# Four buffers of queries, beta added a chunk later, and another split of the product sums in a sparse two-layer graph kernel

## The chip, the cores and the metric

The kernel runs on one core of a Trainium2 chip. The metric is the device time of one execution in microseconds (us), the median of several runs. The core has TensorE (PE) for matmuls and transposes, VectorE (DVE), ScalarE (ACT) and GpSimd (POOL), each with a queue of its own that is worked off in order, and SyncE (SP), which here only issues transfers. POOL also issues the indirect transfers: gathers and scatters whose rows are told by a list of indices.

## The reference

Two layers of graph attention over N = 2048 nodes, for a batch of B = 8 graphs that share one sparse adjacency matrix `adj`, with F = 256 features, H = 4 heads and D = 64 features a head. Cut to what matters:

```python
# layer 0
q, k, v = x @ Wq.T + bq, x @ Wk.T + bk, x @ Wv.T + bv          # split into 4 heads
scores = clip(q . k / sqrt(64), -10, 10); scores = -10 where adj == 0
attn = softmax(scores over each chunk of 256 nodes)              # 8 softmaxes a row
ctx = sum over chunks of attn @ v
y = layernorm(ctx @ Wo.T + bo + x) * gamma + beta
x = layernorm(x + y)
# layer 1
Wh = x @ W;  e = leaky_relu(Wh . a_src [row] + Wh . a_dst [column]), only where adj != 0
x = layernorm(x + elu(softmax(e) @ Wh))
```

A row of `adj` has few entries (up to 24 here), so the kernel gathers the neighbours of each node instead of computing all 2048 scores. The nodes that are not neighbours enter layer 0's softmax only through a constant, which is added in closed form.

## The kernel before, in words

The nodes are sorted by their number of neighbours and cut into NT = 16 tiles of 128 nodes, one node a partition. Tile t has room for `CAPS[t]` neighbours: 24, 14, 13, 12, 11, 11, 10, 10, 9, 9, 8, 8, 7, 7, 6, 5, together 164. The batch is cut into NG = 4 groups of G = 2 graphs. The kernel goes through these stages:

1. The table stage (to about 255 us in the profile): `edge_lists` finds each node's neighbours, while `tables(0, t)` computes keys and values (`kv_d`), queries and x + beta (`qx_d`, both halves of one row) of group 0 and stores them in DRAM.
2. Layer 0 for groups 0 to 3, 16 tiles each, in an order of tiles that goes 15, 13, ..., 1, 0, 2, ..., 14. During groups 0 to 2, `tables(g + 1, t)` makes the next group's tables, one tile at a time.
3. Layer 1 for the first pair of groups, woven into groups 2 and 3 of layer 0.
4. Layer 1 for the second pair, alone at the end.

**A tile of layer 0.** `fetch0` gathers the tile's neighbours. A *unit* is a buffer for UNIT = 2 neighbours of all 128 nodes, with keys in its first 512 columns and values in the next; there is a ring of RING = 14 such buffers (`tag="u"`). Each neighbour is one gather on POOL (L469), and one more (L507) brings the tile's own queries and x + beta into `qx`, of which there are 3 buffers. `scores0` multiplies queries and keys on DVE and sums each product over the features of a head. That sum is made in two ways. For the first `npe` units it goes over PE: DVE makes the product (L530), PE transposes it in eight pieces that add up in PSUM (L541), ACT copies the result (L547), and PE multiplies by a matrix of zeros and ones (L551). For the other units DVE makes the product (L555) and sums it with a reduce (L557). The product of unit i is written over the keys of unit i - 1, whose product was made before; the first unit's has a tile of its own, `prod`. `softmax0` clamps the scores (L571; PE's from PSUM, the others from SBUF), and makes the weights on DVE with one exponential on ACT. `context0` multiplies the values by the weights, most units on DVE (L481), the last quarter on ACT (L487), and sums them over the neighbours on PE (L494), which frees the ring's buffers. `finish0` applies Wo and the first layernorm and adds x + beta, which it reads from `qx` (L619 and L625); after L625 the `qx` buffer is free. `rows1` makes the tile's rows for layer 1.

**Tables.** `chunk_x` (L322) works on two tiles of x at once, every other tile: PE transposes x (L334), ACT copies it out as `xT` and `xC` (L336, L339). The `xt` tile of x, two buffers, then serves a second end: in `tables` of the odd tile POOL adds beta to it in place (L352), and it is stored in `qx_d`. Then it is loaded again by `load_x`, two tiles ahead.

**What sets the order.** The loop from L779 on writes out, for each tile k: the gathers of tile k + 1 (`fetch`), the scores of k, the rest of k - 1 and k - 2, the tables, then softmax and context of k. A planner then puts each engine's instructions in an order, by what it takes to be ready first; so the order on an engine is not that of the source, and a small edit can move many instructions. At run time every engine keeps that order: an instruction that waits holds up what is behind it. On POOL, that means that an add (L352) or a queries gather (L507) that waits holds up the gathers of units behind it.

Of the kernel before, what the change touches and what calls it, by code (L numbers as in the profile page):

```python
# [9 lines left out]
F32 = mybir.dt.float32  # L10
# [4 lines left out]
ALU = mybir.AluOpType  # L15
AX = mybir.AxisListType

P = 128
H = 4
D = 64  # L20
DP = 8
NJ = D // DP
# [14 lines left out]
G = 2  # L37
UNIT = 2
# [133 lines left out]
def sparse_path(ctx: ExitStack, tc: tile.TileContext, keep, x, adj, Wq, bq, Wk, bk, Wv, bv, Wo, bo, gamma, beta, W, a,  # L172
                out):
    nc = tc.nc
    B, N, F = x.shape
# [146 lines left out]
    def chunk_x(g, t):  # L322
# [18 lines left out]
        xTs[g, t] = xT, xC, xt  # L341
        return xT

    def tables(g, t):
        if t % 2 == 0:
            chunk_x(g, t)
        xT, xC, xt = xTs[g, t - t % 2]
        rows = slice(t % 2 * P, (t % 2 + 1) * P)
        if t % 2:

            xv = xt.rearrange("p k (b f) -> p (k b) f", b=G)
            nc.gpsimd.tensor_tensor(xv, xv, beta_r.unsqueeze(1).to_broadcast([P, 2 * G, F]), op=ALU.add)  # L352
            nc.sync.dma_start(qx_d[g][(t - 1) * P:(t + 1) * P, GF:].rearrange("(k p) f -> p k f", p=P), xt)
        kvs = work.tile([P, 2 * GF + 1], F32, tag="kvs", name="kvs", bufs=1)
        if g == PG:
            nc.scalar.copy(kvs[:, 2 * GF:], rank[:, t:t + 1])
        vk = kvs[:, 0:GF].rearrange("p (j b f) -> p b j f", b=G, j=NJ)
        for b in range(G):
            pm = bank("tk")
            for kc in range(KC):  # L360
                nc.tensor.matmul(pm[:, 0:F], xT[:, b * KC + kc, rows], wkv[:, kc, 0:F], start=(kc == 0), stop=False,  # L361
                                 skip_group_check=True)
            add_bias(pm[:, 0:F], biasT[:, 1])
            for kc in range(KC):
                nc.tensor.matmul(pm[:, F:], xC[:, b * KC + kc, rows], wkv[:, kc, F:], start=False, stop=(kc == KC - 1),  # L365
                                 skip_group_check=True)
            nc.scalar.copy(vk[:, b], pm[:, 0:F].rearrange("p (j f) -> p j f", j=NJ))
            nc.scalar.copy(kvs[:, GF + b * F:GF + (b + 1) * F], pm[:, F:])  # L368
        nc.sync.dma_start(kv_d[g][t * P:(t + 1) * P, :], kvs[:, 0:kv_d[g].shape[1]])
        q = bank("tk")  # L370
        for b in range(G):
            qb = q[:, b * F:(b + 1) * F]
            for kc in range(KC):
                nc.tensor.matmul(qb, xT[:, b * KC + kc, rows], wq[:, kc, :], start=(b == 0 and kc == 0), stop=False,  # L374
                                 skip_group_check=True)
            add_bias(qb, biasT[:, 0])
        qs = work.tile([P, GF], F32, tag="qs", name="qs", bufs=1)
        nc.scalar.copy(qs.rearrange("p (j b f) -> p b j f", b=G, j=NJ),
                       q.rearrange("p (b j f) -> p b j f", b=G, j=NJ))
        nc.sync.dma_start(qx_d[g][t * P:(t + 1) * P, 0:GF], qs)  # L380
        if t == NT - 1:

            tot = small.tile([P, G, KC], F32, tag="tot", name="tot", bufs=1)
            nc.vector.tensor_reduce(tot, xsum.pop(g), axis=AX.X, op=ALU.add)
            mv = small.tile([P, KC, G], F32, tag="mvs", name="mvs", bufs=1)
            pv = bank("tk")[:, 0:KC * G].rearrange("p (c b) -> p c b", c=KC)
            for oc in range(KC):
                for kc in range(KC):
                    nc.tensor.matmul(pv[:, oc, :], wkv[:, kc, F + oc * P:F + (oc + 1) * P], tot[:, :, kc],
                                     start=(oc == 0 and kc == 0), stop=(kc == KC - 1), skip_group_check=True)  # L390
            for oc in range(KC):
                nc.scalar.activation(mv[:, oc, :], pv[:, oc, :], AF.Identity, scale=-1.0, bias=bvc[:, oc:oc + 1])
            bO = small.tile([P, G, KC], F32, tag="bO", name="bO")
            po = bank("tk")[:, 0:KC * G].rearrange("p (c b) -> p c b", c=KC)
            for oc in range(KC):
                for kc in range(KC):
                    nc.tensor.matmul(po[:, oc, :], wo[:, kc, oc * P:(oc + 1) * P], mv[:, kc, :],
                                     start=(oc == 0 and kc == 0), stop=(kc == KC - 1), skip_group_check=True)
            for oc in range(KC):
                nc.scalar.activation(bO[:, :, oc], po[:, oc, :], AF.Identity, bias=biasT[:, 2, oc:oc + 1])  # L400
            biasO[g] = bO

    def first_tables(t):
        if t == 0:
            load_x(0, 0)
        if t % 2 == 0 and t + 2 < NT:
            load_x(0, t + 2)
        tables(0, t)

    with tc.tile_pool(name="lists", bufs=1) as pool:  # L410
# [92 lines left out]

    def fetch0(g, t):
        units = gather(kv_d[g].shape[1], kv_d[g], idx, t)
        qx = work.tile([P, 2 * GF], F32, tag="qx", name="qx", bufs=3)
        nc.gpsimd.indirect_dma_start(out=qx, out_offset=None, in_=qx_d[g],  # L507
                                     in_offset=bass.IndirectOffsetOnAxis(ap=node[:, t:t + 1], axis=0))
        got0[g, t] = qx, units

    def scores0(g, t):
# [2 lines left out]
        q = qx[:, 0:GF]  # L514
        sc = small.tile([P, GH, S], F32, tag="sc", name="sc")

        npe = len(units) - len(units) // 3
        ps_sc = bank("tf")[:, 0:GH * S].rearrange("p (s e) -> p s e", e=GH)
        W8 = GH * DP
        qv = q.rearrange("p (k j w) -> p k j w", k=UNIT, w=W8).unsqueeze(3)  # L520
# [1 line left out]
        def product(i):  # L522

            u, s0, n = units[i]
            if i:
                room = units[i - 1][0][:, :, 0:GF]
            else:
                room = work.tile([P, UNIT, GF], F32, tag="prod", name="prod", bufs=1)
            prod = room.rearrange("p k (j w) -> p k j w", w=UNIT * W8)[:, :, :, 0:n * W8]
            nc.vector.tensor_tensor(prod.rearrange("p k j (s w) -> p k j s w", w=W8),  # L530
                                    u[:, :, 0:GF].rearrange("p s (k j w) -> p k j s w", k=UNIT, w=W8),
                                    qv.to_broadcast([P, UNIT, NJ // UNIT, n, W8]), op=ALU.mult)
            return prod

        for i in range(0, npe, 4):
            some = units[i:min(i + 4, npe)]
            pr = bank("pr", 1).rearrange("p (k r) -> p k r", r=P)
            for k, (u, s0, n) in enumerate(some):
                prod = product(i + k)
                for j in range(NJ):  # L540
                    nc.tensor.matmul(pr[0:n * W8, k, :], prod[:, j // (NJ // UNIT), j % (NJ // UNIT), :], ident, is_transpose=True,  # L541
                                     start=(j == 0), stop=(j == NJ - 1), skip_group_check=True)
            m = len(some)
            prT = work.tile([P, 4, P], F32, tag="prT", name="prT", bufs=1)
            full = m - 1 if some[-1][2] < UNIT else m
            if full:
                nc.scalar.copy(prT[:, 0:full, :], pr[:, 0:full, :])  # L547
            if full < m:
                nc.scalar.copy(prT[0:W8, full, :], pr[0:W8, full, :])
            for k, (u, s0, n) in enumerate(some):  # L550
                nc.tensor.matmul(ps_sc[:, s0:s0 + n, :], prT[0:n * W8, k, :], sel[0:n * W8, 0:n * GH],  # L551
                                 start=(s0 == 0), stop=(k == m - 1 and i + m == npe), skip_group_check=True)
        for u, s0, n in units[npe:]:
            prod = u[:, :, 0:GF].rearrange("p s (j w) -> p s j w", w=W8)
            nc.vector.tensor_tensor(prod, prod, q.rearrange("p (j w) -> p j w", w=W8).unsqueeze(1)  # L555
                                    .to_broadcast([P, n, NJ, W8]), op=ALU.mult)
            nc.vector.tensor_reduce(sc[:, :, s0:s0 + n].rearrange("p e s -> p s e"),  # L557
                                    prod.rearrange("p s j (e d) -> p s e j d", d=DP),
                                    axis=AX.XY, op=ALU.add)
        st0[g, t] = ps_sc, sc, min(S, UNIT * npe)  # L560


# [3 lines left out]
    def softmax0(g, t):  # L566
        S = CAPS[t]
        n = GH * S
        ps_sc, sc, sp = st0.pop((g, t))
        for some, dots in ((sc[:, :, 0:sp], ps_sc[:, 0:sp, :].rearrange("p s e -> p e s")), (sc[:, :, sp:], sc[:, :, sp:])):  # L570
            nc.vector.tensor_scalar(some, dots, -10.0, 10.0, op0=ALU.max, op1=ALU.min)  # L571
        e = ebuf[:, 0:n]
        ev = e.rearrange("p (e s) -> p e s", s=S)
        nc.scalar.activation(ev, sc, AF.Exp)
# [198 lines left out]
            (fetch1 if layer else fetch0)(*at(i))  # L773
            fetched[0] += 1

    load_x(1, 0)
    fetch(0)
    waiting = None
    for k, (layer, i) in enumerate(seq):  # L779
# [6 lines left out]
        if layer == 0:  # L786
# [11 lines left out]
            if i:  # L798
                finish0(*at(i - 1))
            if g + 1 < NG:  # L800
                if i % 2 == 0 and i + NT + 2 < NG * NT:
                    load_x((i + NT + 2) // NT, (i + 2) % NT)
                tables(g + 1, i % NT)
            if tables_first:
                fetch(k + 1)
# [449 lines left out]
```

## Time and profile before

| | |
|---|---|
| time, median of 3 runs | 2462.93 us (2452.32 to 2464.49) |
| span of the profiled run | 2573.9 us |
| PE busy | 1940.6 us, 75% |
| DVE busy | 1833.1 us, 71% |
| POOL busy | 1505.4 us, 58% |
| ACT busy | 1408.0 us, 55% |
| mean granted clock of PE | 0.864 of full speed |
| moved by DMA | 669.10 MB, mean 260 GB/s |

The profiled run is longer than the timed ones, so times of the profile are compared with each other, and carried over to the timed runs by the ratio 2462.9 / 2573.9 = 0.957. A line of groups names the source line, the engine, the operation, what it writes and reads, the count, then the busy time in us and the mean of one instruction in ns, then the idle time of the engine just before such instructions and what ended it. A line of waits reads: who waited, for what, us in total, times, the longest.

### The profile page before, as it was taken

To read this page: it belongs to the slowest core of one execution; us is meant where nothing else is said; L and a number is where in the kernel's file an instruction comes from. 1 tells how busy PE (TensorE), PEld (TensorE's weight loads), DVE (VectorE), ACT (ScalarE), POOL (GpSimd) and SP (SyncE) were. 2 spreads that over 40 slices of the span, in tenths; PEclk is the share of its full clock that TensorE was granted. 3 is DMA by queue.
4 is the path that set the end of the run, shared out by engine and by line. 5 is a ranking of instruction groups with operands and counts; after the bars stand their busy time and mean duration, and the time that the engine had idled before them with its cause. 6 is when DMAs were issued, how large, how long until landed. Compare 5 with 4: busy or idle time off the path is not lost. (4 is left out here: it accounts for less than half of the span.)

```text
span 2573.9 us, 38911 instructions
## 1 busy us (share of the span) xinstructions
PE 1940.6 (75%) x11946; PEld 1657.1 (64%) x11946; DVE 1833.1 (71%) x4071; ACT 1408.0 (55%) x5011; POOL 1505.4 (58%) x1225
## 2 busy tenths in 40 slices
PE   6787787688878879989888877775856786555764
PEld 5675676577666767777777765664756675444654
DVE  5865567767557777767878797776877877656765
ACT  3573353355545455555555665654454567556756
POOL 1123655475545655655677667566757753667764
PEclk9888897898899999899999988886977887777877
DMA  6744977497877868887769878867769874986763
GB/s 217 261 154 159 330 254 256 149 336 254 292 259 243 279 221 307 294 299 271 264 239 369 293 276 299 302 230 250 230 212 338 306 260 178 346 306 236 279 243 108
DMA packets 240749, 669.10 MB, mean 260 GB/s; under 512 B 44455, under 2 KB 70826, under 8 KB 238486
## 3 DMA queue, kind: packets, MB, share of 16 engines
q0 software_dynamic: 156800, 505.01, 56.8%
q1 hardware_dynamic: 80016, 151.56, 16.1%
q10 hardware_dynamic: 3718, 9.97, 1.2%
q8 instruction: 98, 1.61, 0.2%
q14 instruction: 117, 0.96, 0.1%
HBM read 612.79 MB, written 126.36 MB: 287 GB/s over the span
## 5 line engine op out<-in xcount | busy, mean ns | idle before, releaser
L469 POOL DMA_INDIRECT u<-kv_d,idx x656 | 829.1, 1264 | 348.7 <-PE acc L494 161.0
L494 PE MATMUL acc<-ident,u 128*128 128x128 f32 x5248 | 745.0, 299 | 200.0 <-DVE u L481 97.0
L494 PEld LDWEIGHTS acc<-ident,u 128*128 128x128 f32 x5248 | 666.8, 156 | 267.1 <-DVE u L481 137.9
L469 POOL DMA_INDIRECT u<-wh_d,idx x328 | 402.6, 1228 | 166.0 <-issue 77.4
L481 DVE TENSOR_TENSOR u<-u,al 128x1024 f32<-128x1024 f32 x280 | 337.2, 1238 | 1.2
L481 DVE TENSOR_TENSOR u<-u,z 128x1024 f32<-128x1024 f32 x266 | 314.8, 1214 | 0.8
L487 ACT ACTIVATE u<-u,z 128x64 f32<-128x64 f32 x1008 | 259.0, 336 | 24.9 <-DVE z L678 10.6
L541 PE MATMUL pr<-ident,u 128*128 128x128 f32 x1472 | 208.7, 291 | 55.7 <-DVE u L530 49.3
L530 DVE TENSOR_TENSOR u<-u,qx 128x1024 f32<-128x1024 f32 x184 | 228.7, 1243 | 26.4 <-DMA u<-kv_d,idx 20.8
L541 PEld LDWEIGHTS pr<-ident,u 128*128 128x128 f32 x1472 | 179.0, 150 | 76.1 <-DVE u L530 64.3
L487 ACT ACTIVATE u<-u,al 128x64 f32<-128x64 f32 x800 | 206.9, 341 | 34.6 <-DVE al L585 15.2
L641 PE MATMUL mf<-wa,x1T 128*128 128x264 f32 x512 | 172.4, 465 | 63.0 <-issue 19.9
L352 POOL TENSOR_TENSOR xt<-xt,beta_r 128x1024 f32<-128x1024 f32 x32 | 80.2, 2508 | 217.0 <-PE tk L334 178.1
L507 POOL DMA_INDIRECT qx<-qx_d,node x64 | 81.4, 1272 | 185.6 <-DVE o L625 114.8
L361 PE MATMUL tk<-wkv,xT 128*128 128x256 f32 x512 | 154.6, 418 | 21.3 <-ACT xC L339 14.9
L641 PEld LDWEIGHTS mf<-wa,x1T 128*128 128x128 f32 x512 | 102.2, 221 | 103.8 <-issue 41.2
L374 PE MATMUL tk<-wq,xT 128*128 128x256 f32 x512 | 146.8, 404 | 28.1 <-ACT kvs L368 20.9
L613 PE MATMUL mf<-wo,cT 128*128 128x256 f32 x512 | 145.5, 408 | 6.3 <-ACT whs L644 4.5
L365 PE MATMUL tk<-wkv,xC 128*128 128x256 f32 x512 | 147.4, 404 | 0.0
L435 ACT ACTIVATE sq<-o,nm 128x256 bf16<-128x256 f32 x256 | 129.5, 506 | 5.0
L619 DVE CUSTOM_DVE_ANT_0 o<-mf,qx 128x256 f32<-128x256 f32 x128 | 49.2, 420 | 104.7 <-PE mf L311 93.9
L712 PE MATMUL mf<-ident,hT 128*128 128x128 f32 x256 | 51.4, 333 | 95.6 <-DVE xr L716 42.8
(168 smaller groups left out, 3434.5 us busy)
## 6 DMA issues: line engine op xcount, KB each, us to landing
kv_d<-kvs SPq DMA_DIRECT2D x48, 512.0 KB
wh_d<-whs SPq DMA_DIRECT2D x64, 260.0 KB
xt<-in_x_dram SPq DMA_DIRECT2D x64, 256.0 KB
qx_d<-xt SPq DMA_DIRECT2D x32, 512.0 KB
qx_d<-qs SPq DMA_DIRECT2D x64, 256.0 KB
x_d<-o SPq DMA_DIRECT2D x64, 256.0 KB
xr<-x_d SPq DMA_DIRECT2D x32, 512.0 KB
u<-kv_d,idx POOLq DMA_INDIRECT x656
```

Of the source, the lines that this page charges most:

```text
L361: nc.tensor.matmul(pm[:, 0:F], xT[:, b * KC + kc, rows], wkv[:, kc, 0:F], start=(kc == 0), stop=False, skip_group_check=True)
L365: nc.tensor.matmul(pm[:, F:], xC[:, b * KC + kc, rows], wkv[:, kc, F:], start=False, stop=(kc == KC - 1), skip_group_check=True)
L374: nc.tensor.matmul(qb, xT[:, b * KC + kc, rows], wq[:, kc, :], start=(b == 0 and kc == 0), stop=False, skip_group_check=True)
L435: nc.scalar.activation(sq, src[:, k, :], AF.Square, bias=nm[:, k:k + 1], accum_out=m2[:, k:k + 1])
L469: nc.gpsimd.indirect_dma_start(out=u[:, k, 0:width], out_offset=None, in_=table, in_offset=bass.IndirectOffsetOnAxis(ap=idx[:, t, s0 + k:s ...
L481: nc.vector.tensor_tensor(pv, pv, av, op=ALU.mult)
L487: nc.scalar.activation(pe, pe, AF.Copy, scale=al[:, e, s0 + k:s0 + k + 1])
L494: nc.tensor.matmul(acc[:, c, :], part[:, k, c * P:(c + 1) * P], ident, is_transpose=True, start=first and k == 0 and c == 0, stop=last and ...
L530: nc.vector.tensor_tensor(prod.rearrange("p k j (s w) -> p k j s w", w=W8), u[:, :, 0:GF].rearrange("p s (k j w) -> p k j s w", k=UNIT, w=W8),
L541: nc.tensor.matmul(pr[0:n * W8, k, :], prod[:, j // (NJ // UNIT), j % (NJ // UNIT), :], ident, is_transpose=True, start=(j == 0), stop=(j ...
L613: nc.tensor.matmul(po[:, b, :], cT[:, b * KC + kc, :], wo[:, kc, :], start=(b == 0 and kc == 0), stop=False, skip_group_check=True)
L641: nc.tensor.matmul(pw[:, 0:F + 2 * H], xT[:, b * KC + kc, :], wa[:, kc, :], start=(kc == 0), stop=(kc == KC - 1))
```

## The change

Four edits:

- `qx` has 4 buffers instead of 3.
- beta is added to a chunk of x when the next chunk begins (`add_beta`, called in `tables` two tiles later; the group's last chunk in its own last tile), where PE's transposes of that chunk lie further back. The load of the chunk after that is now issued in the same place, behind the add and its store.
- The first unit of each tile always has its product sums on DVE, so the tile `prod` is not needed any more; its 4 KB in each partition are those of the fourth `qx` buffer.
- The share of units whose sums DVE makes, a third before, is half in groups 0 and 1 (which have the tables beside them and no layer 1), and a sixth, at least one, in groups 2 and 3. The clamp of DVE's scores is split accordingly, since they now lie at both ends.

```diff
+    def add_beta(g, t):
+        xt = xTs.pop((g, t))[2]
+        xv = xt.rearrange("p k (b f) -> p (k b) f", b=G)
+        nc.gpsimd.tensor_tensor(xv, xv, beta_r.unsqueeze(1).to_broadcast([P, 2 * G, F]), op=ALU.add)
+        nc.sync.dma_start(qx_d[g][t * P:(t + 2) * P, GF:].rearrange("(k p) f -> p k f", p=P), xt)
+
     def tables(g, t):
         if t % 2 == 0:
+            if t:
+                add_beta(g, t - 2)
+            if g * NT + t + 2 < NG * NT:
+                load_x(*divmod(g * NT + t + 2, NT))
             chunk_x(g, t)
         xT, xC, xt = xTs[g, t - t % 2]
         rows = slice(t % 2 * P, (t % 2 + 1) * P)
-        if t % 2:
-            xv = xt.rearrange("p k (b f) -> p (k b) f", b=G)
-            nc.gpsimd.tensor_tensor(xv, xv, beta_r.unsqueeze(1).to_broadcast([P, 2 * G, F]), op=ALU.add)
-            nc.sync.dma_start(qx_d[g][(t - 1) * P:(t + 1) * P, GF:].rearrange("(k p) f -> p k f", p=P), xt)
+        if t == NT - 1:
+            add_beta(g, t - 1)
...
-        qx = work.tile([P, 2 * GF], F32, tag="qx", name="qx", bufs=3)
+        qx = work.tile([P, 2 * GF], F32, tag="qx", name="qx", bufs=4)
...
-        npe = len(units) - len(units) // 3
+        npe = 1 + len(units) - (len(units) // 2 if g < NG // 2 else max(1, len(units) // 6))
...
             u, s0, n = units[i]
-            if i:
-                room = units[i - 1][0][:, :, 0:GF]
-            else:
-                room = work.tile([P, UNIT, GF], F32, tag="prod", name="prod", bufs=1)
+            room = units[i - 1][0][:, :, 0:GF]
...
-        for i in range(0, npe, 4):
+        reduced(*units[0])
+        for i in range(1, npe, 4):
...
-        for u, s0, n in units[npe:]:
-...
+        for unit in units[npe:]:
+            reduced(*unit)
...
-        for some, dots in ((sc[:, :, 0:sp], ps_sc[:, 0:sp, :].rearrange("p s e -> p e s")), (sc[:, :, sp:], sc[:, :, sp:])):
-            nc.vector.tensor_scalar(some, dots, -10.0, 10.0, op0=ALU.max, op1=ALU.min)
+        nc.vector.tensor_scalar(sc[:, :, UNIT:sp], ps_sc[:, UNIT:sp, :].rearrange("p s e -> p e s"), -10.0, 10.0, op0=ALU.max,
+                                op1=ALU.min)
+        for some in [sc[:, :, 0:UNIT]] + ([sc[:, :, sp:]] if sp < S else []):
+            nc.vector.tensor_scalar(some, some, -10.0, 10.0, op0=ALU.max, op1=ALU.min)
```

The calls of `load_x` in `first_tables` and in the main loop (`load_x(1, 0)`, and the one at even tiles) are gone, since `tables` makes them.

## The prediction

> **What bounds the kernel now.** I read the page's busy shares first, then the windows cut where the layer 0 groups end (context copy L604: the 16th ends at 618 us, the 32nd at 1011, the 48th at 1521, the 64th at 2124), then the waits, the groups of instructions, and the landings behind the waits. Columns of a window are PE, PE weight load, DVE, ACT, POOL, clock, DMA share, GB/s.
>
> ```profile
> PE 1940.6 (75%) x11946; PEld 1657.1 (64%) x11946; DVE 1833.1 (71%) x4071; ACT 1408.0 (55%) x5011; POOL 1505.4 (58%) x1225
> 255.00:618.00 363.00, 283.35 (x1731) 242.07 (x1730) 242.91 (x449) 161.85 (x594) 211.06 (x172) 0.86 0.76 259
> 618.00:1011.00 393.00, 329.04 (x2054) 280.66 (x2053) 274.63 (x562) 202.57 (x793) 226.87 (x177) 0.93 0.78 269
> 1011.00:1521.00 510.00, 442.66 (x2848) 379.50 (x2846) 388.34 (x824) 293.27 (x1083) 337.21 (x253) 0.94 0.82 293
> 1521.00:2124.00 603.00, 433.18 (x2770) 373.24 (x2771) 469.01 (x1002) 336.12 (x1228) 394.37 (x313) 0.82 0.77 267
> ```
>
> Over the whole span no engine is full, but the stages differ. PE is busy 78%, 84% and 87% in groups 0, 1 and 2, which also hold the tables of the next group; DVE 67%, 70% and 76%. In group 3, without tables, DVE leads, 78% against 72%. So PE is the fuller engine before 1521 us and DVE after it, and both run in order, each with a fifth of its time lost to the other. The page's chain covers only the last 13 us and says nothing here.
>
> ```profile
> POOL u L469 <- PE acc L494: 223.1, 89, 19.0
> POOL xt L352 <- PE tk L334: 178.1, 11, 22.5
> POOL qx L507 <- DVE o L625: 114.8, 20, 19.1
> DVE prod L530 <- DMA qx<-qx_d,node: 26.1, 10, 9.7
> DVE prod L530 <- DMA u<-kv_d,idx: 25.4, 5, 10.7
> DVE u L530 <- DMA u<-kv_d,idx: 20.8, 10, 5.3
> ```
>
> POOL issues all gathers in order and waits at three places: for a ring buffer that PE frees (223 us), for the transposes ahead of x + beta (178 us) and for a queries buffer (115 us). But of the 178 us, the trace places seven waits (122 us) before 170 us, in the table stage, where POOL has nothing else to do. Only some 26 us of DMA lateness at queries and some 46 at units reach DVE's first products. POOL is not the bound; what it delays sometimes is.
>
> [...] 1243 ns for the product (L530), 1212 for the reduce (L557). A reduce thus costs as much as a multiply. [...] gathers with a DVE multiply beside most of them took 1.59 us on average, those with none 1.00. The change leaves the number of such multiplies alone. [...]
>
> **The change, part by part.** A group has 16 tiles and 86 units (12, 7, 7, 6, 6, 6, 5, 5, 5, 5, 4, 4, 4, 4, 3, 3). Before, a third of them, rounded down, is reduced on DVE: 24, and 62 go over PE. After, half, rounded down, in groups 0 and 1: 39 on DVE, 47 on PE. In groups 2 and 3 it is one a tile and two for the largest: 17 on DVE, 69 on PE.
>
> ```profile
> L541 PE MATMUL pr<-ident,u 128*128 128x128 f32 x1472 | 208.7, 291 | 55.7 <-DVE u L530 49.3 <-issue 5.8
> L541 PE MATMUL pr<-ident,prod 128*128 128x128 f32 x512 | 76.8, 290 | 48.9 <-DVE prod L530 39.2 <-issue 8.7 <-PE mf L641 0.8
> L551 PE MATMUL tf<-sel,prT 128*128 128x16 f32 x496 | 73.8, 278 | 29.8 <-ACT prT L547 18.4 <-issue 11.1
> L557 DVE TENSOR_REDUCE sc<-u 128x16 f32<-128x1024 f32 x64 | 77.4, 1212 | 0.2
> L557 DVE TENSOR_REDUCE sc<-u 128x8 f32<-128x512 f32 x32 | 21.8, 680 | 0.1
> ```
>
> PE, a unit: (208.7 + 76.8 + 73.8) us over 248 units is 1.45 us. The product is made on DVE on either path, so a unit moved to DVE adds only its reduce, 1.21 us (0.68 for a half unit). Groups 0 and 1, each: PE -15 x 1.45 = -21.8 us. DVE before 16 x 1.21 + 8 x 0.68 = 24.8, after 32 x 1.21 + 7 x 0.68 = 43.5, so +18.7, and a third clamp (L571's small form, 178 ns) in 14 tiles, +2.5: +21. That brings PE to 262 and 307 us and DVE to 264 and 296: level. Groups 2 and 3, each: PE +7 x 1.45 = +10.2. DVE saves little, since the last half units were the cheap ones: 17 x 1.21 = 20.6 instead of 24.8, -4.2. ACT gets four more copies of sums a group at 0.58 us; ACT is 58% busy and they lie beside products.
>
> What of this is on the path? Bounds: nothing, if each engine waits for the other as before; all, if PE alone set the time. I take half of PE's relief in groups 0 and 1, because DVE becomes as full: -22 us together (bounds 0 and -44). In group 2, at 87% PE, I take 7 of the 10 us; in group 3 PE has 170 us idle and DVE leads, so +1. Sum: -14 us.
>
> Four queries buffers: the wait L507 <- L625 goes for most tiles. In the order of the changed program most queries gathers have no DVE instruction left to wait for, and the first tiles' stand four together, then 39 units where 29 stood. Behind L507 on POOL are the next units; behind these DVE's first product. The ring keeps its 14 buffers, so POOL soon waits there instead, and the gain is only the lateness that reached DVE: 26 us of queries plus some part of the units'.
>
> x + beta a chunk later: the wait of L352 for the transposes of its own chunk goes. Orders compared: before, an add that waits for PE in groups 0 to 2 needs an instruction 8 to 67 places (median 18) ahead of the one that the next gather needs anyway; after, 8 to 148 (median 74). So it was mostly the ring's wait under another name. Three adds still stand ahead of the first gather, on the same transposes, so the start (first gather at 255.6 us although the first ring buffer is cleared at 224) stays. The load of x now goes out after the add and its store, but a buffer of x had to be stored before its reload already, and there are two as before; the order on SP in the table stage is the same. Cost nothing, hidden by PE's tables. The add itself, 2.4 us, stays.
>
> Without its own tile, the first unit's product takes its neighbour's room: no bytes, no time; the bytes pay for the queries buffer. But the first unit is now multiplied and reduced (2.45 us) before DVE makes PE's first product. PE can do tables, contexts and outputs meanwhile in groups 0 to 2.
>
> For queries and units together DVE waits 89 us on landings in these four stages by the trace, 17 of them at the start, which stay. Of the other 72 I take 30 as gone and two thirds of these as time: -20 (bounds 0 and -72). In all -34 us of the profiled 2574; the timed run is 2463, a factor 0.957: -32. **2463 - 32 = 2431 us.**
>
> **Rivals.** *Nothing to measure.* For: the ring sets POOL's lead before and after, and PE's relief equals DVE's load, 21.8 against 21. Against: PE is 11 to 14 points fuller in groups 0 and 1. Only some 8 us remain: 2455.
>
> *The late gathers were the path.* For: at tile t = 0 of group 0, L352 held POOL 18 us and DVE then waited 9.7 for queries, in a step of 60 us where group 1 takes 44. Against: 72 us is all that DVE waits there on landings. All 72, and PE's balance entire (-44 + 20): -96 x 0.957 = -92: 2371.
>
> *Slower.* PE's first product is later by 2.45 us in each of 64 tiles, 157 us; PE already waits for DVE's products (49.3 + 39.2 us above). In groups 2 and 3 PE gets 20 us more, and with no reduce left after PE's last product, DVE has less of its own to do while sums return. Against: the planner's order in the changed program puts other DVE work there (more of it than before in groups 1 and 2). If a quarter of the 157 shows, 39, and 10 in group 2, less 22 won: +27 x 0.957: 2489.
>
> **How the numbers follow.** Forecast 0.53, nothing 0.15, late gathers 0.12, slower 0.20. The threshold of 0.5% is 2451 and 2475. The forecast's own spread, -14 to -60 us, is faster throughout: faster 0.65, same 0.15, slower 0.20. The range goes from 2385, short of the centre of the late-gather case, to 2480, half of the slower one; about 2 in 10 lie outside.
>
> **What would show it.** Right: PE busy down by about 22 us in each of groups 0 and 1 and up by 10 in each of 2 and 3; 98 full reduces of 1.21 us and 14 half ones; L507's wait under 30 us in all and the ring's wait up by much of what goes; DVE's waits for queries near zero; groups 0 and 1 shorter by 10 to 20 us each, group 2 not shorter by PE work. Wrong: PE's waits for the first transposes grow by more than 30 us; the ring's wait stays while groups shrink (then POOL mattered more); groups 2 and 3 move by over 20 us (then the new order of the instructions, not these costs, decides).

## The result, and the profile after

The changed kernel takes 2430.6 us (median of 4 runs, 2418.3 to 2439.9) against 2463.7 us (2452.3 to 2473.2) before: a ratio of 0.986, 95% interval 0.981 to 0.991, or 33 us less. The forecast was 2431. Ratios here and below are of runs within 1.5% of the fastest of the same kernel; three of the later profiles (*head_qx*, *split_qx* and *split_beta*) are of slower runs, so times read in them are rough.

The profiled run of before that the prediction reads took 2573.9 us, 110 us more than the timed ones. The kernel before was profiled once more, unchanged, and that run took 2464.4 us; it is the one to set beside the 2438.2 us of the profile after, and it is called *control* from here on. Busy shares first, of control and then of after:

```profile
PE 1895.6 (77%) x11946; PEld 1622.3 (66%) x11946; DVE 1835.0 (74%) x4071; ACT 1404.5 (57%) x5011; POOL 1523.2 (62%) x1225
```

```profile
PE 1885.9 (77%) x11786; PEld 1610.9 (66%) x11786; DVE 1853.9 (76%) x4117; ACT 1400.3 (57%) x5029; POOL 1496.6 (61%) x1225
```

PE does 160 matmuls less and is busy 10 us less, DVE does 46 instructions more and is busy 19 us more. Neither comes near the 33 us of the result.

Next the windows, cut at the context copy of each group's 16th tile (L604 before, L613 after). Columns as in the prediction; the first number after the bounds is the window's length. Control, then after; groups 0 to 3, then the rest.

```profile
256.60:672.90 416.30, 341.88 (x2126) 291.21 (x2126) 293.09 (x558) 199.11 (x739) 263.14 (x210) 0.90 0.81 281
672.90:1075.80 402.90, 346.94 (x2207) 295.98 (x2206) 300.35 (x607) 220.23 (x864) 247.92 (x189) 0.94 0.80 282
1075.80:1505.50 429.70, 382.62 (x2525) 330.29 (x2523) 354.62 (x753) 261.51 (x954) 296.27 (x220) 0.95 0.83 299
1505.50:2023.10 517.60, 384.24 (x2540) 332.54 (x2541) 428.80 (x915) 309.85 (x1137) 372.83 (x294) 0.85 0.83 291
2023.10:2464.00 440.90, 256.46 (x1675) 224.65 (x1673) 294.25 (x728) 283.48 (x989) 284.52 (x236) 0.77 0.70 247
```

```profile
257.30:669.60 412.30, 339.23 (x1998) 285.21 (x1998) 308.65 (x597) 196.01 (x741) 259.64 (x208) 0.87 0.82 288
669.60:1065.50 395.90, 345.03 (x2095) 292.30 (x2094) 313.70 (x639) 221.40 (x873) 238.99 (x188) 0.91 0.80 283
1065.50:1491.70 426.20, 380.57 (x2530) 328.52 (x2528) 347.47 (x732) 258.78 (x955) 287.88 (x226) 0.94 0.85 305
1491.70:1999.10 507.40, 380.75 (x2615) 334.52 (x2615) 423.86 (x911) 308.14 (x1136) 366.92 (x289) 0.88 0.83 292
1999.10:2438.00 438.90, 253.49 (x1673) 219.82 (x1671) 293.74 (x729) 285.68 (x1000) 283.51 (x235) 0.77 0.70 249
```

The 26 us between these two profiles come in small pieces from everywhere: 4, 7, 3.5, 10 and 2 us. The largest piece is in group 3, which has no tables and where the change gave PE *more* work. The groups of instructions of after, counted by form (busy us, mean ns, then the idle time ahead):

```profile
L543 DVE TENSOR_REDUCE sc<-u 128x16 f32<-128x1024 f32 x98 | 118.4, 1211 | 0.3
L543 DVE TENSOR_REDUCE sc<-u 128x8 f32<-128x512 f32 x14 | 9.5, 676 | 0.0
L553 PE MATMUL pr<-ident,u 128*128 128x128 f32 x1712 | 250.6, 295 | 64.3 <-DVE u L534 54.9 <-issue 7.9 <-PE mf L650 0.8
L553 PE MATMUL pr<-ident,u 128*64 128x128 f32 x144 | 21.4, 285 | 0.0
L563 PE MATMUL tf<-sel,prT 128*128 128x16 f32 x428 | 63.1, 272 | 18.4 <-ACT prT L559 18.2
L563 PE MATMUL tf<-sel,prT 64*128 64x8 f32 x36 | 7.1, 269 | 0.0
L580 DVE TENSOR_SCALAR sc<-sc 128x16 f32<-128x16 f32 x74 | 13.3, 185 | 0.1
```

Now 112 reduces cost 127.9 us where 96 cost 99.2, and PE's part costs 250.6 + 21.4 + 63.1 + 7.1 = 342.2 us where it cost 354.5 in control (209.6 + 74.5 + 70.4). PE's idle time ahead of the transposes fell to 64.3 us, from 54.7 + 46.4 = 101.1. The waits on POOL, of control and then of after (us in total, times, longest):

```profile
POOL xt L352 <- PE tk L334: 179.5, 11, 25.0
POOL u L469 <- PE acc L494: 177.0, 106, 13.5
POOL qx L507 <- DVE o L625: 81.0, 16, 11.7
```

```profile
POOL u L475 <- PE acc L500: 258.3, 108, 21.3
POOL xt L348 <- PE tk L334: 159.3, 10, 24.1
POOL qx L513 <- DVE o L634: 28.7, 10, 11.2
```

The wait for a queries buffer fell by 52 us, the add's by 20, and the wait for the ring grew by 81: together POOL waits slightly longer at these three places (446 us against 438).

### The profile page after: what moved, and what is told of

It reads as the page before. It is cut to its first block, busy times and chain, and to the rows that moved or that the text cites. A ratio compares the mean times of both kernels' runs of the same rounds, so it can differ in the third digit from the quotient of the medians.

```text
span 2438.2 us, 38640 instructions
## 1 busy us (share of the span) xinstructions
PE 1885.9 (77%) x11786; PEld 1610.9 (66%) x11786; DVE 1853.9 (76%) x4117; ACT 1400.3 (57%) x5029; POOL 1496.6 (61%) x1225
## 5 line engine op out<-in xcount | busy, mean ns | idle before, releaser
L475 POOL DMA_INDIRECT u<-kv_d,idx x656 | 814.6, 1242 | 402.6 <-PE acc L500 213.0
L500 PE MATMUL acc<-ident,u 128*128 128x128 f32 x5248 | 719.3, 293 | 195.3 <-DVE u L487 125.6
L500 PEld LDWEIGHTS acc<-ident,u 128*128 128x128 f32 x5248 | 642.0, 152 | 258.4 <-DVE u L487 170.8
L475 POOL DMA_INDIRECT u<-wh_d,idx x328 | 407.8, 1243 | 137.1 <-issue 64.9
L553 PE MATMUL pr<-ident,u 128*128 128x128 f32 (+1 forms) x1856 | 270.2, 294 | 64.3 <-DVE u L534 54.9
L534 DVE TENSOR_TENSOR u<-u,qx 128x1024 f32<-128x1024 f32 (+1 forms) x232 | 278.2, 1199 | 21.2 <-DMA u<-kv_d,idx 20.2
L553 PEld LDWEIGHTS pr<-ident,u 128*128 128x128 f32 (+1 forms) x1856 | 230.5, 151 | 91.2 <-DVE u L534 73.9
L493 ACT ACTIVATE u<-u,z 128x64 f32<-128x64 f32 x1008 | 259.6, 337 | 28.7 <-DVE z L687 26.4
L541 DVE TENSOR_TENSOR u<-u,qx 128x1024 f32<-128x1024 f32 (+1 forms) x112 | 132.4, 1187 | 52.3 <-DMA u<-kv_d,idx 28.2
L513 POOL DMA_INDIRECT qx<-qx_d,node x64 | 76.8, 1201 | 96.2 <-DVE o L634 28.7
L543 DVE TENSOR_REDUCE sc<-u 128x16 f32<-128x1024 f32 (+1 forms) x112 | 127.8, 1144 | 0.3
```

The costliest lines, as they stand in the source:

```text
L475: nc.gpsimd.indirect_dma_start(out=u[:, k, 0:width], out_offset=None, in_=table, in_offset=bass.IndirectOffsetOnAxis(ap=idx[:, t, s0 + k:s ...
L493: nc.scalar.activation(pe, pe, AF.Copy, scale=al[:, e, s0 + k:s0 + k + 1])
L500: nc.tensor.matmul(acc[:, c, :], part[:, k, c * P:(c + 1) * P], ident, is_transpose=True, start=first and k == 0 and c == 0, stop=last and ...
```

## The experiments

Twelve runs. The first four shared one chip, on which before takes 2469.7 us. The others ran where the same program takes some 6% longer, 2618 us (the next four) and 2627 us (the last four), so ratios to before are compared, not times.

**Nothing changed.** *control* is before without an edit.

> The kernel before, unchanged. Every theory expects a ratio of 1 within 0.5%. It gives the scatter of the comparison and a second profile of the kernel before, since its first profile (2574 us) lay 110 us above its timed runs (2463); I expect this profile's span nearer to 2463 us and the stages shorter than in the first by the same few per cent, without a change in which engine is the fuller one.

Measured: 2471.5 us, ratio 1.001 (0.999 to 1.003). A difference of 0.5% is measurable here, and the windows above are a fair base.

**Each part alone, with three queries buffers.** *head* puts the first unit on DVE in place of one of its others, so that both engines keep as many units as before; *split* has the new shares; *beta* has only the later beta, on the kernel before.

```diff
# head
-        npe = len(units) - len(units) // 3
+        npe = 1 + len(units) - len(units) // 3
# split
+        npe = 1 + len(units) - (len(units) // 2 if g < NG // 2 else max(1, len(units) // 6))
# head and split, both
+        reduced(*units[0])
-        for i in range(0, npe, 4):
+        for i in range(1, npe, 4):
...
# beta
+            if t:
+                add_beta(g, t - 2)
+            if g * NT + t + 2 < NG * NT:
+                load_x(*divmod(g * NT + t + 2, NT))
```

> As before, but DVE's third of the units includes the first unit of each tile, so that the separate product tile is gone; the counts on PE and DVE stay, three query buffers, beta as before. Slower rival: PE's first product is 2.45 us later in each tile, so +20 to +40 us and longer waits of PE for the first product. Forecast's theory: within 10 us of before. In 14 of 16 tiles one more clamp, 2.5 us a group on DVE.

> Of the change the new split of the product sums alone (first unit on DVE, no tile of its own for the product; half on DVE in groups 0 and 1, a sixth in groups 2 and 3); three query buffers, and beta as before. Forecast's theory: 14 us off (-0.5%), PE about 22 us less in each of groups 0 and 1. Late gathers theory: no gain, 0 to +10 us. Theory that the planner's order decides: anything within 30 us either way, not to be told from counts.

> Of the change the later beta alone (added at the next chunk, load of x behind it), three query buffers, split as before. Forecast's theory: 0 us (within 8), because the add's wait is mostly the ring's wait under another name; POOL's wait at the add falls and its wait for the ring grows by as much. Late gathers theory: 20 us or more off.

Measured: head 1.0125 (1.009 to 1.016), split 1.011 (1.007 to 1.014), beta 1.011 (1.007 to 1.014): each 25 to 27 us *slower*. For all three the prediction booked a gain or nothing, and each is a loss by itself. By stage the losses are not spread out as a cost in every tile would be. Length in us:

| | to first gather | group 0 | group 1 | group 2 | group 3 | rest |
|---|---|---|---|---|---|---|
| control | 256.6 | 416.3 | 402.9 | 429.7 | 517.6 | 441.3 |
| after | 257.3 | 412.3 | 395.9 | 426.3 | 507.3 | 439.1 |
| head | 252.1 | 422.4 | 401.1 | 468.4 | 507.0 | 435.1 |
| split | 250.5 | 416.9 | 423.6 | 445.4 | 511.6 | 439.8 |
| beta | 253.5 | 419.8 | 412.0 | 454.1 | 514.3 | 440.3 |

All three lose 16 to 39 us in group 2, and within it most at one tile, the largest (t = 0, 12 units, the ninth in order). From the context copy before to its own it takes 51 us in control and 47 in after, but 70 in head, 68 in split and 70 in beta. The timeline of that step shows a wait that goes with it in two of them. In split, POOL first, then DVE (start, us busy, engine, line, in brackets the idle time before and what ended it):

```profile
1281.97 0.99 POOL L469 DMA_INDIRECT u<-kv_d,idx  x1 [0.30 <-DMA u<-kv_d,idx]
1283.27 0.99 POOL L469 DMA_INDIRECT u<-kv_d,idx  x1 [0.30 <-issue]
1284.56 0.95 POOL L507 DMA_INDIRECT qx<-qx_d,node  x1 [0.30 <-issue]
```

```profile
1278.50 0.16 DVE L448 TENSOR_TENSOR nm<-nm,r 128x2 f32<-128x2 f32 x1
1289.78 2.36 DVE L535 TENSOR_TENSOR u<-u,qx 128x1024 f32<-128x1024 f32 x2 [11.11 <-DMA qx<-qx_d,node]
```

POOL gathers the tile's 24 neighbours one after the other, 1.3 us each, and the queries last. DVE, which needs the queries for the very first product, stands idle for 11 us, and no wait of POOL's is to be seen: the "issue" in brackets says that it waited for nothing. The wait comes from the gather's place in POOL's fixed order: DVE's last read of a queries buffer before it (L628) had ended at 1275.3 us, and still seven gathers of units, from 1275.49 to 1283.27 us, started ahead of it. In beta the same gather comes last as well, and DVE waits 15.6 us:

```profile
1293.12 1.23 DVE L536 TENSOR_TENSOR prod<-u,qx 128x1024 f32<-128x1024 f32 x1 [15.56 <-DMA qx<-qx_d,node]
```

In control it stands ten gathers ahead of the last unit's:

```profile
1254.67 1.96 POOL L469 DMA_INDIRECT u<-kv_d,idx  x1 [0.30 <-DVE u L481]
1256.93 0.97 POOL L507 DMA_INDIRECT qx<-qx_d,node  x1 [0.30 <-issue]
1258.21 0.99 POOL L469 DMA_INDIRECT u<-kv_d,idx  x1 [0.30 <-PE acc L494]
```

In after it stands 28 gathers ahead of the last unit's, so ahead of all the tile's units:

```profile
1205.97 1.71 POOL L513 DMA_INDIRECT qx<-qx_d,node  x1 [5.03 <-DVE o L634]
```

Neither control nor after has a wait for queries in that step. The same tile of group 0 shows the same thing with other kernels. There control and beta have the queries last, DVE waits 9.8 and 9.6 us for them, and the step takes 60.5 and 64.2 us. In head, split and after the gather stands 10 or 11 places ahead, and the step takes 47.7, 51.4 and 54.6 us.

Head has the late queries too, but there DVE waits 17.6 us before that for something else, a part of the tables that the planner had put ahead of the tile's scores. That step and the group's first (20 us in control, 35 in head) make up 34 of head's 39 us in group 2. For split's 21 us in group 1 I found no such single place.

**With the fourth queries buffer.** On the slower chip: *head_qx* and *split_qx* are head and split with four buffers, *split_beta* is the whole change with three, *qx_beta* the whole change with the old share of a third.

```diff
# head_qx, split_qx, qx_beta; split_beta keeps 3
-        qx = work.tile([P, 2 * GF], F32, tag="qx", name="qx", bufs=3)
+        qx = work.tile([P, 2 * GF], F32, tag="qx", name="qx", bufs=4)
```

> The kernel head (DVE's third includes the first unit, no product tile) with four query buffers; beta as before. Theory that the fourth buffer carries the gain: 30 to 60 us faster than head, so 0 to 30 us faster than before. Theory that the planner's order of the instructions decides: no pattern, anywhere within 35 us of before. Forecast's theory: 20 us faster than head.

> The whole change without the later beta: split and four query buffers. Fourth-buffer theory: as fast as the whole change, 25 to 40 us faster than before, since the later beta costs or gives nothing. If the later beta is needed as well: 0 to 15 us slower than before. Order theory: no pattern.

> The whole change with three query buffers instead of four. Fourth-buffer theory: 20 to 30 us slower than before, like each of the two alone, with POOL's wait for a query buffer at 100 us or more. Additive theory: 27 + 26 = 53 us slower. Order theory: no pattern. Forecast's theory: 14 us faster than before.

> The whole change but for the shares: a third of the units on DVE in all groups as before, the first unit among them; four query buffers and the later beta. If the shares carry little: within 10 us of the whole change, so 25 us or more faster than before. Forecast's theory: 18 us faster than before (the shares being worth 14 of 32). Order theory: no pattern.

Measured: head_qx 1.006 (1.002 to 1.010), split_qx 1.000 (0.998 to 1.003), split_beta 1.017 (1.010 to 1.023), qx_beta 1.013 (1.008 to 1.017). In all four-buffer kernels the queries gather of the large tile in group 2 stands 28 places ahead of the last unit's, in all three-buffer kernels but control one place behind it. The step takes 53 us in head_qx, 46 in split_qx, 52 in qx_beta, and 75 in split_beta. But the place of this gather does not settle the time of the kernel, nor even that of the step. qx_beta has four buffers, the early gather and the shorter step, and is 1.3% slower than before. And in *after_again*, the next run, the step takes 61 us with the gather early; the longest wait of DVE in it is for PE's sums, and it is the longest of its row:

```profile
DVE sc L577 <- PE tf L563: 77.9, 21, 12.5
```

The fourth buffer alone was not run: in this change the product tile's 4 KB are what pays for it.

**The whole change again, and its best part.** Where before takes 2627 us: *after_again* is the whole change, *split_qx_again* the change without the later beta.

> The whole change, once more and with more rounds, beside the other kernels of this call. If the gain is the change's own: a ratio of 0.98 to 0.99 on this chip too. If the chip decides [...]: 0.99 to 1.005.

> The whole change without the later beta, beside the whole change. Fourth-buffer theory: within 0.4% of the whole change. If the later beta is needed as well, or the order that goes with it: 1% or more slower than the whole change.

Measured: 0.994 (0.991 to 0.997) and 1.000 (0.997 to 1.003). The gain is there on this chip as well, but it is 0.6% and not 1.4%. The change without the later beta is 0.6% slower than the whole change, between the two expectations, and the intervals just touch. With three buffers the later beta did not help: split has 1.011 without it on one chip and 1.017 with it on the other, which the intervals do not tell apart. So the parts do not add up. All that was measured, as ratios to before:

| | 3 buffers | 4 buffers |
|---|---|---|
| before | 1.001 | not run |
| later beta alone | 1.011 | not run |
| first unit on DVE, a third | 1.0125 | 1.006 * |
| first unit, new shares | 1.011 | 1.000 *, 1.000 * |
| first unit, a third, later beta | | 1.013 * |
| first unit, new shares, later beta | 1.017 * | 0.986, 0.994 * |

(* on the slower chip.) Of the parts that were measured in more than one pair of kernels, two have the same sign in all pairs. The fourth buffer has -0.7%, -1.1% and -2.2%; only the last pair was measured on one chip. The new shares have -0.15% and -0.6%, with intervals that overlap, and -1.9% from qx_beta to after_again, some 49 us on one chip. So qx_beta, which was to show whether the shares carry little, says the opposite: with the buffer and the later beta in place they count about as much as the buffer.

**Is it the tables that crowd the step?** In the three-buffer kernels PE also does 4 to 4.5 tables of group 3 within that step, in control and the four-buffer ones 1 to 2. A rival to the late queries was therefore that these tables hold up the sums. *split_hold_g3* is split with an edge in the order: PE may begin a table of group 3 no more than two tiles ahead of its own place. *after_hold2* puts that edge on the whole change, for the tables of groups 1 to 3, to see whether a stricter order beats both kernels.

```diff
-            summed(acc, u[:, :, GF:2 * GF], s0 == 0, s0 + n == S)
+            done = summed(acc, u[:, :, GF:2 * GF], s0 == 0, s0 + n == S)
+        ends.append(done.ins)
...
-                tables(g + 1, i % NT)
+                with tc.issue_after(ends[i - 2]):      # split_hold_g3: g == 2 only
+                    tables(g + 1, i % NT)
```

> The new split alone (three query buffers, beta as before), but PE's part of the tables of group 3 may stand at most two tiles ahead of their own place, by an edge that orders instructions and waits for nothing. Work, buffers and the order of groups 0 and 1 stay those of the split alone. Theory that the order decides, through four tables packed into the largest tile's step of group 2: that step falls from 68 us to 50 or so, the ratio from 1.011 to 1.005 or less. Theory that the three buffers themselves cost it: the step stays near 68 us, the ratio near 1.011.

> The whole change with that edge for the tables of groups 1 to 3: PE's part of a table stands at most two tiles ahead of its own place. It should also free the start: the eight tables of group 1 ahead of the first context go, POOL's adds no longer stand ahead of the first gather, and the first gather comes at 225 us instead of 257. Order theory: 10 to 30 us faster than the whole change. Against: the eight tables have to be made later, when PE is at 80% and more, some 8 x 5 us, which would eat the gain; then within 10 us of the whole change.

Measured: split_hold_g3 1.024 (1.018 to 1.029), after_hold2 1.019 (1.014 to 1.024). In split_hold_g3 the tables within the step fell from about 4 to between 1 and 2, and the step still took 64 us, with the queries still the last gather and 8.9 us of DVE waiting for them, the longest of its row (us in total, times, longest):

```profile
DVE u L538 <- DMA qx<-qx_d,node: 21.9, 11, 8.9
```

So the crowding theory, which put the step at some 50 us and the ratio at 1.005, does not hold as it stood. What share the tables have in the step stays open: split itself was not run on this chip, and the edge moved other instructions too. For after_hold2 the first gather came at 220 us instead of 261, as it should, but only 6 of these 41 us were left at the end of group 0 and 18 at the end of group 1; then groups 2 and 3 and the rest each took longer by 23, 23 and 14 us than in after_again. Why was not settled. No version beat the changed kernel.

## Why the prediction was right or wrong

**The time was right, its composition was not.** The sum had -14 us for the shares, -20 for the queries and the late gathers, and nothing for the later beta and for the first unit. In the runs, moving the first unit with the old third costs 27 us, the later beta alone 26, and the new shares on top of the first unit win nothing with three buffers (1.011 against 1.0125), 0.6% with four, and 1.9% with four and the later beta. The -34 is met by a combination whose parts were each mis-sized. That the total came out to 1 us is luck (on the slower chip the same change won 14 us), and it should not be read as a confirmation of the terms.

**The engines' costs were right for one instruction, too large for groups 0 and 1.** 98 full reduces at 1211 ns and 14 half ones at 676 ns; the third clamp 185 ns against 178. PE's transposes and sums by group: 95.5 to 77.2 us and 82.8 to 70.1 us in groups 0 and 1, 85.2 to 93.9 and 86.7 to 98.5 in groups 2 and 3: -18 and -13 where -22 was said, +9 and +12 where +10 was. DVE rose by 16 and 13 us in groups 0 and 1 against +21.

**"PE busy down by about 22 us in each of groups 0 and 1" failed**, although most of that work went. PE busy fell by 2.7 and 1.9 us. In group 0 PE's other matmuls took longer in the same number: those that make the rows for layer 1 41.5 us instead of 36.6 (112 each), those that apply Wo 37.5 instead of 33.1 (120 each). The clock is the reason. The trace's record of the granted clock has two levels only, full and half, and a mean of 0.872 (control: 0.898) says how they are mixed. In groups 0, 1 and 3 of after a row matmul took 402 to 410 ns on average when it started at full clock and 655 to 670 at half; in group 0, 41 of the 112 started at half clock after the change and 20 in control, and of Wo's 120 it was 26 and 4. In group 1 (0.914 instead of 0.941) the row matmuls took 4 us longer in the same way, but most of the saving went to tables: the planner moved 32 matmuls for keys and values into it, 76.1 us instead of 63.9, and out of group 2. That is also why group 2, where +10 was said, was busy 2 us less. Group 3, where +10 was said too, was busy 3.5 us less: there 20 of 128 row matmuls started at half clock instead of 47. So the -22 of the sum was half of a relief that came to less than 5 us of busy time.

**"Groups 0 and 1 shorter by 10 to 20 us each" failed**: 4 and 7. Group 3, booked at +1, gave 10.

**The windows were cut in the wrong places.** The ends given for the groups (618, 1011, 1521 us) lie before the copies they name; in the first profile the 16th, 32nd and 48th context copies are at 693, 1116 and 1569 us. The reading that rested on it holds with the right ends all the same: PE busy 80%, 84% and 86% in groups 0 to 2, DVE 78% against 71% in group 3.

**The queries' waits.** L507's wait under 30 us in all: 28.7. The ring's wait up "by much of what goes": up 81 us. "DVE's waits for queries near zero" failed: 32.6 us in control, 24.1 after.

```profile
DVE u L541 <- DMA u<-kv_d,idx: 28.2, 9, 13.4
DVE u L541 <- DMA qx<-qx_d,node: 24.1, 10, 4.1
```

Two kinds of lateness hide in that row. In after no wait for queries is longer than 4.1 us. In split, beta, split_beta and split_hold_g3 the same row has one of 9 to 16 us at the large tile of group 2. In head the wait for the tables hides it, and control, with three buffers as well, has its longest, 9.8 us, at that tile of group 0. For queries and units together in groups 0 to 3, DVE waited 90.4 us in control and 72.5 after: 18 us gone, where the sum had 30. (The 89 us that the sum started from also hold 11 us of waits for layer 1's gathers; without these the first profile has 78.) The step put the worth of the fourth buffer in the wait it takes away. Its worth was larger: against the same kernel with three, the whole change gains 2.2% by it, some 59 us, more than the whole result. One thing that comes with it is seen in the traces: the planner sets the queries gather ahead of the units, presumably because it has less to wait for. How much of the 59 us that place gives is not shown, since no run moved this gather alone. POOL was busy 58% in the first profile, and the wait that went, 52 us from control to after, came back at the ring, 81 us more.

**"Cost nothing" for the later beta failed.** With the later beta alone, the kernel is 26 us slower, 24 of them in group 2, where DVE waited 15.6 us for queries. The edit did not even shorten the wait that it was made for: in beta the add's wait rose by 11 us, and the ring's stayed (177.0 us in control, 174.8 in beta).

```profile
POOL xt L348 <- PE tk L334: 191.0, 11, 22.0
```

What is left to explain the loss is the planner's new order; this is argued and not shown, since no run changed the order and nothing else. The prediction named it among what could make it wrong ("the new order of the instructions, not these costs, decides") and gave it no number.

**The rivals.** *Slower* rested on PE's first product coming 2.45 us later in each of 64 tiles. Head is the test and is slower by 27 us, near the 27 of that rival. But PE's idle time ahead of its transposes is 90.4 us in head and 64.3 in after, against 101.1 in control, so it fell where it was feared to grow by more than 30; and head's loss lies in two tile steps of group 2 rather than in all tiles. The number was met, the mechanism was not seen. *Late gathers* at -92 and *nothing* at -8 were not met; on the slower chip the result, -14 us, lies nearer to the second.

**Open.** Why the later beta helps only with four buffers and the new shares; why the shares are worth 1.9% there and nothing in split; what split loses in group 1; why the ordered versions lose in groups 2 and 3; and how much of the 33 us belongs to any one edit. Shown is a wait of 9 to 16 us for late queries at the largest tile, in four of the three-buffer experiments, and its absence there in all kernels with four. That this wait is what the three-buffer kernels lose is not shown.

## What to carry to other kernels

Where a planner orders in-order queues, look up the place of the one small gather that every product needs: here, behind 24 others, it idled the consumer for 9 to 16 us, and the producer's row of waits showed nothing. A buffer more may let such a gather move forward. Test each edit of a set by itself before crediting the sum, and with the others present too: here each of three parts alone lost 1%, and all four together won 1.4% on one chip and 0.6% on another. And a sum that agrees with the clock is no proof of its terms.

## What the runs showed of the hardware that was not expected

**Less work on PE, lower granted clock.** From control to after, PE's instructions in group 0 fell by 6% (2126 to 1998) and its busy time by 0.8%, because more of the other matmuls started at half clock (of the 112 for rows 41 instead of 20). In group 1 the mean clock was 0.914 instead of 0.941, in group 3, with more work, 0.882 instead of 0.855. Head, with PE's share unchanged, has 0.895 and 0.949 in groups 0 and 1, split, with the smaller one, 0.885 and 0.907. Beta, which takes nothing from PE, also has a lower clock there (0.878 and 0.921), so this is a pattern and not a proof.

**Not every half-clock stretch follows a long gap.** In groups 0 to 3 of after, PE was at half clock at the end of an idle gap, or went to it within 7 us, for all 32 gaps of 2.5 us and more, for 15 of the 21 of 1.5 to 2.5 us, and for 9 of the 22 of 1 to 1.5 us. Of the 49 half-clock stretches that began there, 31 have a gap of 2.5 us or more in the 7 us before they begin, and 45 have one of 1.5 us or more, where 31% of all moments in these groups have one. Half clock goes with gaps here, and short ones belong to the count. But 4 stretches have none of 1.5 us, and no run changed the gaps alone: what sets the clock was not settled.

**Chips differ.** The kernel before takes 2470 us on one chip and 2618 to 2627 us where the later runs were made, where the mean clock of the profiled runs is 0.85 rather than 0.88, and the ratio of the change differs too (0.986, and 0.994 with an interval that ends at 0.997).
